# Local attention layers: output projection of two units at once over 256 columns, the norm's squares in the tile of the scaled rows, another order of the step

## The chip, the cores and the metric

The kernel runs on one core of one Trainium2 chip. The time is device microseconds of one execution of the whole program; lower is better. The core has TensorE (PE, matmuls, with its weight loads shown as PEld), VectorE (DVE), ScalarE (ACT), GpSimd (POOL) and SyncE (SP), whose queue issues most of the DMAs.

## The reference

The program computes a chain of blocks on x of 16 samples x 128 tokens x 128 features, all in float32. The change lies in one of them, `_L0_ffn_ref`, a stack of six layers of local attention and feed-forward:

```python
for i in range(DEPTH):                                  # DEPTH = 6
    x = attn_layer(shift_tokens(x), Wqkv[i], q_scale[i], k_scale[i], Wo[i]) + x
    x = ffn_layer(shift_tokens(x), ln_g[i], ln_b[i], W1[i], b1[i], W2[i], b2[i]) + x

def attn_layer(x, Wqkv, qs, ksc, Wo):
    q, k, v = jnp.split(x @ Wqkv, 3, -1)                # 16 heads of 64
    q = l2norm(sh(q)) * qs;  k = l2norm(sh(k)) * ksc    # then rotary with a scale
    out = local_attention(q, k, v)                      # windows of 32, softmax(8 q k + mask)
    return out.transpose(0, 2, 1, 3).reshape(b, n, INNER) @ Wo

def ffn_layer(x, g, bln, W1, b1, W2, b2):
    xn = (x - mu) / jnp.sqrt(var + 1e-05) * g + bln
    a, gate = jnp.split(xn @ W1 + b1, 2, -1)            # 341 each
    return a * jax.nn.gelu(gate) @ W2 + b2
```

`shift_tokens` moves the upper half of the features down by one token. Before this stack stand a conditioned attention and a warp of the images, behind it a diffusion step, a gated linear attention and two mixtures of experts; none of them is touched.

## The kernel before

x lies transposed in SBUF as `xs`: features on the 128 partitions, the 16 samples and their tokens along the row. The shift costs nothing, since the upper 64 partitions are read one column further on (`Local.halves`). A **unit** (`Unit`) is one sample in one layer, so there are 6 x 16 = 96. A **feed-forward** (`FeedForward`) takes four samples at once, 512 columns.

What a unit does, piece by piece, with the lines of the profile:

- `project(k,c)` (L774): half of the queries (k = 0) or keys (k = 1), 512 columns, from `xs` by the layer's `wqkv`. Each is read by `square` (L779, ACT, into `sq`) and `cossin` (L787, DVE, times cosine and sine into `t`); `sum_squares` (L797, DVE), `lengths` (L803 and the power of L804, POOL), `rotate` (two adds at L811, POOL, into `rot`) and `normalize_keys` (L816, POOL) follow.
- `transpose(k,c)` (L838, PE) and `keep_transpose` (L843, ACT) bring four pairs of heads into `qkT`.
- `scores(half)` (L855, PE, eight heads, into a tile of the ring "s"), `mask` (L862, DVE, in place), `maxima` (the reduction of L869 and a small multiply at L874 of 128x8 by 128x8, both in SBUF; DVE), `exponentials` (L882, ACT, one ACTIVATE per head), `normalize` (reciprocal L889 on DVE, multiply L890 on POOL).
- `values(c)` (L823, PE) with `keep_values` (L830, ACT).
- `turn(i)` (L896, PE, transposes four heads of `pe`) with `keep_turn` (L903, into `pT`: on ACT for i = 1, else on DVE), `weigh(half)` (L910, PE), `keep_weighed(half)` (L918, ACT, into `oT`), then `out` (L926, PE, eight matmuls of 128 columns that add up) and `add` (L934, DVE, two adds of 64x128 into `xs`). Every float32 matmul is two instructions in the trace, a transpose is one.

The feed-forward: `mean` (L947, PE), `center` (L951, DVE, into `xc`), `square` (L957, ACT, into `sqc`), `variance` (L963, PE), `root` (L970 on DVE, the power of L971 on POOL), `spread` (two DMAs on SP: four roots per token go to DRAM and come back broadcast to all partitions), `scale` (L985, DVE, into `xn`), `up(c)` (L993, PE), `gelu(c)` (L1001, ACT), `gate(c)` (L1009, DVE), `down` (L1017, PE) and `add` (L1023, DVE).

Psum is handed out in two rings by `Local.ps`: "s", two tiles of 1024 columns, for the scores, and "g", four tiles of 512 columns, for everything else. The tiles of a ring are given out in the order of the calls, so a piece that takes a "g" tile waits until the tile four calls earlier has been read. SBUF tiles of one name go round in the same way, with the number of buffers that the first argument of `tile` gives (`xc`, `xn`, `sqc`: one; `oT`, `v`, `qkT`, `ge`: two; `pe`, `pT`: four).

The order is written out by hand: with `manual_schedule` for PE, DVE, ACT and POOL, every engine gets its instructions in the order in which the pieces are called. `STEP` (L1031) lists the pieces of one step and `run_layers` (L1117) calls it once per four units. In a step that starts at unit n, p0 to p3 are units n to n+3, t0 to t3 are units n-2 to n+1, o0 to o3 are units n-3 to n; f is the feed-forward of the four samples before (`mean`, `center`, `square`), and e, g and h are the one of eight units before (`variance` to `scale`; `up`, `gelu`, `gate`; `down`, `add`). So a unit passes through two steps and a feed-forward through two. `FIRST` (L1075) is the list for n = 0. The DMAs of SP and the DMA waits lie outside of the written order.

## Time and profile before

| | us |
|---|---|
| three runs | 2558.02, 2558.49, 2556.04; median 2558.02 |
| the profiled execution, its own time | 2561.24 |
| its span in the profile | 2559.3 |
| first and last `out` matmul (L926) of the local layers | 494.0 and 2208.2 |
| one step in the middle of the layers | 71.0 |

Some groups of instructions between 650 and 2220 us (count, mean ns of one):

| line, engine, what | count | mean ns |
|---|---|---|
| L926 PE matmul, 128 columns | 1392 | 275 |
| L934 DVE add, 64x128 | 174 | 279 |
| L918 ACT copy into `oT`, 128x512 | 174 | 601 |
| L957 ACT square into `sqc`, 128x512 | 22 | 679 |
| L874 DVE multiply, 128x8 | 172 | 786 |
| table load ahead of L1001 and of L882, ACT | 22 and 22 | 1283 |
| L804 POOL power, 128x32 | 85 | 5676 |
| L890 POOL multiply, 128x1024 | 172 | 1897 |

How to read it: the mean ns of one matmul is its whole passage, and matmuls overlap, so the pace of PE is read from the distance between starts or from the chain of waits. A line of the profile's windows or groups counts an engine as busy while an instruction is in it, also when that instruction only waits inside. The profiled execution is 3 us above the median of the runs.

### The profile page before, as it was taken

To read this page: it belongs to the slowest core of one execution; us is meant where nothing else is said; L and a number is where in the kernel's file an instruction comes from. 1 tells how busy PE (TensorE), PEld (TensorE's weight loads), DVE (VectorE), ACT (ScalarE), POOL (GpSimd) and SP (SyncE) were. 2 spreads that over 40 slices of the span, in tenths; PEclk is the share of its full clock that TensorE was granted. 3 is DMA by queue.
4 is the path that set the end of the run, shared out by engine and by line. 5 is a ranking of instruction groups with operands and counts; after the bars stand their busy time and mean duration, and the time that the engine had idled before them with its cause. 6 is when DMAs were issued, how large, how long until landed. Compare 5 with 4: busy or idle time off the path is not lost.

```text
span 2559.3 us, 47602 instructions
## 1 busy us (share of the span) xinstructions
PE 2427.9 (95%) x17644; PEld 1671.2 (65%) x17644; DVE 2210.8 (86%) x2961; ACT 1925.6 (75%) x5717; POOL 1999.7 (78%) x1242
## 2 busy tenths in 40 slices
PE   7999998899999999999999999999999999789998
PEld 5676765566666666666666666666666766456766
DVE  5899998899999989999999989999899998455544
ACT  4788887688888878888888888888888888344422
POOL 3777777899999989999999999999999999243210
PEclk9999999999999999999999999999999999899999
DMA  3111113000000000100001000100000000022220
GB/s 107 29 31 32 28 31 109 13 1 6 13 30 16 6 13 1 38 8 6 13 8 38 6 13 1 38 8 6 5 5 5 5 6 1 11 77 68 85 71 25
DMA packets 89487, 64.73 MB, mean 25 GB/s; under 512 B 56802, under 2 KB 75944, under 8 KB 88488
## 3 DMA queue, kind: packets, MB, share of 16 engines
q1 hardware_dynamic: 78280, 37.56, 5.9%
q0 software_dynamic: 9216, 22.03, 2.8%
q8 instruction: 140, 2.29, 0.4%
q10 hardware_dynamic: 1760, 2.10, 0.2%
q14 instruction: 91, 0.75, 0.1%
HBM read 55.06 MB, written 6.60 MB: 24 GB/s over the span
## 4 chain that ended last, share of the span: by engine, by line
PE 55%; DVE 11%; ACT 6%; issue 1%; POOL 1%; DMA 1%; DVEq 0%; POOLq 0%; ACTq 0%; SPq 0%
PE g L774 9%; PE s L855 6%; PE g L910 5%; PE g L838 5%; PE g L993 5%; PE g L823 4%; PE g L896 4%; PE g L926 4%; ACT pe L882 3%; DVE t L787 2%; DVE nm L869 2%; PE e L1531 2%; DVE ss L797 1%; PE o L1549 1%; DVE nm L874 1%
## 5 line engine op out<-in xcount | busy, mean ns | idle before, releaser
L882 ACT ACTIVATE pe<-s,nm,r 128x128 f32<-128x128 f32 x1536 | 683.2, 485 | 2.4 <-DVE nm L874 1.8
L804 POOL TENSOR_TENSOR r<-ss,power 128x32 f32<-128x32 f32 x96 | 543.7, 5663 | 8.0
L811 POOL TENSOR_TENSOR rot<-t 128x512 f32<-128x512 f32 x384 | 481.9, 1276 | 20.8 <-DVE t L787 20.6
L787 DVE TENSOR_TENSOR t<-g,tab 128x1024 f32<-128x1024 f32 x372 | 447.0, 1215 | 38.9 <-PE g L774 28.5
L890 POOL TENSOR_TENSOR pe<-pe,den 128x1024 f32<-128x1024 f32 x192 | 363.2, 1897 | 49.5 <-DVE den L889 46.2
L774 PE MATMUL g<-wqkv,xs 128*128 128x512 f32 x744 | 377.5, 606 | 0.6 <-DVE t L787 0.4
L882 ACT ACTIVATION_READ_ACCUMULATOR pe<-s,nm,r 128x1 f32 x1536 | 356.4, 232 | 0.0
L779 ACT ACTIVATE sq<-g 128x512 f32<-128x512 f32 x372 | 223.9, 609 | 94.1 <-PE g L774 84.0
L843 ACT COPY qkT<-g 128x512 f32<-128x512 f32 x384 | 219.9, 614 | 61.3 <-PE g L838 60.7
L862 DVE TENSOR_TENSOR s<-s,band 128x1024 f32<-128x1024 f32 x192 | 234.6, 1222 | 16.7 <-PE s L855 16.2
L838 PEld LDWEIGHTS g<-ident,rot 128*128 128x128 f32 x1536 | 175.1, 142 | 105.4 <-issue 44.7
L896 PEld LDWEIGHTS g<-ident,pe 128*128 128x128 f32 x1536 | 179.7, 141 | 98.4 <-issue 86.8
L838 PE MATMUL g<-ident,rot 128*128 128x128 f32 x1536 | 226.3, 281 | 16.1 <-ACT qkT L843 9.1
L869 DVE TENSOR_REDUCE nm<-s 128x8 f32<-128x1024 f32 x192 | 232.7, 1212 | 0.9
L797 DVE TENSOR_REDUCE ss<-sq 128x16 f32<-128x1024 f32 x192 | 231.5, 1206 | 2.4 <-ACT sq L779 0.3
L855 PE MATMUL s<-qkT,qkT 64*128 64x128 f32 x3072 | 223.1, 285 | 3.8 <-ACT qkT L843 1.9
L855 PEld LDWEIGHTS s<-qkT,qkT 64*128 64x128 f32 x3072 | 186.3, 187 | 61.8 <-issue 51.5
L896 PE MATMUL g<-ident,pe 128*128 128x128 f32 x1536 | 223.0, 276 | 0.9 <-POOL pe L890 0.9
L903 DVE COPY pT<-g 128x512 f32<-128x512 f32 x288 | 192.5, 682 | 16.8 <-PE g L896 13.0
L823 PE MATMUL g<-wqkv,xs 128*128 128x512 f32 x384 | 203.1, 611 | 0.0
L910 PE MATMUL g<-pT,v 128*64 128x128 f32 x3072 | 199.8, 277 | 0.8 <-DVE pT L903 0.8
L926 PEld LDWEIGHTS g<-oT,wo 128*128 128x128 f32 x1536 | 182.7, 192 | 23.4 <-issue 16.7
(341 smaller groups left out, 4799.9 us busy)
## 6 DMA issues: line engine op xcount, KB each, us to landing
wqkv<-in_lo_wqkv_dram SPq DMA_DIRECT2D x6, 1536.0 KB
roots<-lo_roots SPq DMA_DIRECT2D x24, 256.0 KB
fr_image<-xres SPq DMA_DIRECT2D x32, 104.0 KB
wo<-in_lo_wo_dram SPq DMA_DIRECT2D x6, 512.0 KB
box<-fr_image,idx POOLq DMA_INDIRECT x128
fr_moved<-out SPq DMA_DIRECT2D x16, 128.0 KB
w<-in_lo_w_dram SPq DMA_DIRECT2D x6, 341.0 KB
wqk<-in_a_wqk_dram ACTq DMA_DIRECT2D x4, 256.0 KB
```

The lines of the kernel that those rows point to most:

```text
L774: self.nc.tensor.matmul(pq, self.xT, self.w.qkv[:, at : at + 512], start=True, stop=True)
L787: self.nc.vector.tensor_tensor(self.t[k][:, :, 8 * c : 8 * c + 8, :], heads(self.bank["q", k, c]).unsqueeze(1).to_broadcast([P, 2, 8, 64]) ...
L804: self.nc.gpsimd.tensor_tensor(self.r, self.ss, self.lo.power, ALU.pow)
L811: self.nc.gpsimd.tensor_tensor(self.rot[k][:, :, at], t[:, 0, :, at], t[:, 1, :, other], ALU.add)
L823: self.nc.tensor.matmul(pv, self.xT, self.w.qkv[:, 2048 + c * 512 : 2560 + c * 512], start=True, stop=True)
L838: self.nc.tensor.transpose(pt[:, j * P : j * P + P], flat[:, at : at + P], self.s.ident)
L855: self.nc.tensor.matmul(sc[:, k * 512 + j * P : k * 512 + j * P + P], self.T[0][rows, pr, :], self.T[1][rows, pr, :], start=True, stop=True,)
L882: self.nc.scalar.activation(self.pe[half][:, h, :], sc3[:, h, :], AF.Exp, bias=self.nm[half][:, h : h + 1], scale=self.r[:, hd : hd + 1], ...
L890: self.nc.gpsimd.tensor_tensor(pe, pe, den.unsqueeze(2).to_broadcast([P, 8, P]), ALU.mult)
L896: self.nc.tensor.transpose(pt[:, j * P : j * P + P], self.pe[i // 2][:, 4 * (i % 2) + j, :], self.s.ident)
L910: self.nc.tensor.matmul(po[rows, j * P : (j + 1) * P], self.v[:, hd * 64 : hd * 64 + 64], self.pT[2 * half + k][:, j, :], start=True, stop ...
L926: self.nc.tensor.matmul(self.pout[:, 0:P], self.w.o[:, c, :], self.oT[:, c, :], start=(c == 0), stop=(c == 7),)
```

## The change

`out` and `add` move from the unit to a new class `Pair` of two units: `oT` gets a place for both units (8 x 2 x 128 columns instead of 8 x 128), `out` runs eight matmuls of 256 columns, and `add` writes 64x256. `FeedForward.square` puts its squares into the tile `xn`, which `scale` writes later; `sqc` is gone. `STEP` is replaced as a whole; x0 is the pair of units n-4 and n-3, x1 that of n-2 and n-1. 

```diff
@@ -913,25 +913,35 @@
                 )
 
     def keep_weighed(self, half):
-        if half == 0:
-            self.oT = self.lo.tile(2, "oT", [P, 8, P])
+
+        pair = self.pair
+        if pair.oT is None:
+            pair.oT = self.lo.tile(2, "oT", [P, 8, 2, P])
         self.nc.scalar.copy(
-            self.oT[:, 4 * half : 4 * half + 4, :].rearrange("p c t -> p (c t)"),
-            self.bank["o", half],
-        )
+            pair.oT[:, 4 * half : 4 * half + 4, self.b % 2, :],
+            self.bank["o", half].rearrange("p (c t) -> p c t", c=4),
+        )
+
+
+class Pair:
+
+
+    def __init__(self, lo, w, b):
+        self.lo, self.nc, self.w, self.b, self.oT = lo, lo.nc, w, b, None
 
     def out(self):
         self.pout = self.lo.ps("g")
         for c in range(8):
             self.nc.tensor.matmul(
-                self.pout[:, 0:P], self.w.o[:, c, :], self.oT[:, c, :],
-                start=(c == 0), stop=(c == 7),
+                self.pout[:, 0:256], self.w.o[:, c, :],
+                self.oT[:, c].rearrange("p i t -> p (i t)"), start=(c == 0), stop=(c == 7),
             )
 
     def add(self):
-        for rows, x in self.lo.halves(self.b, 1):
-            x = x.rearrange("p i t -> p (i t)")
-            self.nc.vector.tensor_tensor(x, self.pout[rows, 0:P], x, ALU.add)
+        for rows, x in self.lo.halves(self.b, 2):
+            self.nc.vector.tensor_tensor(
+                x, self.pout[rows, 0:256].rearrange("p (i t) -> p i t", i=2), x, ALU.add
+            )
 
 
 class FeedForward:
@@ -953,7 +963,7 @@
         )
 
     def square(self):
-        self.sq = self.lo.tile(1, "sqc", [P, 512])
+        self.sq = self.xn = self.lo.tile(1, "xn", [P, 512])
         self.nc.scalar.activation(self.sq, self.xc, AF.Square)
 
     def variance(self):
@@ -981,7 +991,6 @@
         )
 
     def scale(self):
-        self.xn = self.lo.tile(1, "xn", [P, 512])
         self.nc.vector.tensor_tensor(
             four(self.xn), self.roots.rearrange("p t i -> p i t"), four(self.xc), ALU.mult
         )
...
 STEP = """
-t0.transpose(1,0) p0.project(0,0) t0.keep_transpose(1,0) p0.cossin(0,0) t0.transpose(0,0)
-p0.project(0,1) p0.project(1,0) t0.keep_transpose(0,0) p0.square(0,0) p0.square(1,0)
-p0.cossin(0,1) p0.square(0,1) t0.scores(0) t1.transpose(0,0) t1.keep_transpose(0,0)
-t1.transpose(0,1) t1.keep_transpose(0,1) o0.turn(1) p0.cossin(1,0) t0.mask(0) o0.turn(3)
-t0.transpose(1,1) o0.keep_turn(1) o0.keep_turn(3) t0.transpose(0,1) t0.values(0)
-t0.keep_transpose(1,1) t0.maxima(0) o0.turn(0) o0.keep_turn(0) o0.turn(2) t0.keep_transpose(0,1)
-p0.project(1,1) o0.keep_turn(2) p0.cossin(1,1) p0.sum_squares(0) t0.keep_values(0) t0.values(1)
-e.variance() t0.scores(1) e.root() t0.exponentials(0) t0.mask(1) p0.square(1,1) p0.rotate(0)
-o0.weigh(0) t0.normalize(0) o0.weigh(1) t0.keep_values(1) t1.transpose(1,0) o0.keep_weighed(0)
-o0.keep_weighed(1) p1.project(0,0) t1.keep_transpose(1,0) p1.square(0,0) t0.maxima(1)
-p0.rotate(1) o0.out() p0.sum_squares(1) p1.project(0,1) p1.cossin(0,0) o0.add() t1.values(0)
-p1.cossin(0,1) e.spread() t0.exponentials(1) o1.turn(0) o1.keep_turn(0) p1.square(0,1)
-t1.scores(0) t1.keep_values(0) e.scale() t1.transpose(1,1) t1.keep_transpose(1,1) t1.mask(0)
-o1.turn(1) p1.sum_squares(0) o1.keep_turn(1) g.up(2) t1.maxima(0) g.gelu(2) g.up(1) g.gelu(1)
-t1.scores(1) g.gate(2) o1.weigh(0) p0.lengths() g.gate(1) t0.normalize(1) t1.mask(1) g.up(0)
-p1.project(1,0) t1.maxima(1) o1.keep_weighed(0) g.gelu(0) p1.project(1,1) p1.square(1,0)
-p0.normalize_keys() g.gate(0) p1.square(1,1) o1.turn(3) p1.cossin(1,0) p1.rotate(0)
-p1.cossin(1,1) h.down() o1.keep_turn(3) t2.transpose(0,0) t2.transpose(1,0) h.add()
-t1.exponentials(0) p1.sum_squares(1) p2.project(1,0) p2.square(1,0) p2.project(1,1) p1.rotate(1)
-p1.lengths() t2.keep_transpose(0,0) t1.normalize(0) t2.transpose(0,1) p2.cossin(1,0)
-t2.keep_transpose(1,0) p2.square(1,1) t2.keep_transpose(0,1) p2.cossin(1,1) t2.transpose(1,1)
-o1.turn(2) t2.keep_transpose(1,1) o1.keep_turn(2) t2.scores(0) t2.values(0) t1.exponentials(1)
-p2.project(0,0) t2.mask(0) o1.weigh(1) t2.keep_values(0) p2.cossin(0,0) t1.normalize(1)
-t1.values(1) p2.project(0,1) p2.square(0,0) o1.keep_weighed(1) t1.keep_values(1)
-p1.normalize_keys() t2.maxima(0) t3.transpose(0,0) p2.sum_squares(1) t2.scores(1) p2.square(0,1)
-o2.turn(0) p2.cossin(0,1) p2.rotate(0) t2.values(1) t2.mask(1) t3.keep_transpose(0,0)
-t2.exponentials(0) o2.keep_turn(0) t2.keep_values(1) o2.turn(1) t2.maxima(1) o2.keep_turn(1)
-o1.out() t2.normalize(0) o1.add() t3.transpose(1,0) o2.turn(3) t3.keep_transpose(1,0) o2.turn(2)
-t3.transpose(0,1) t3.scores(0) t2.exponentials(1) p2.sum_squares(0) o2.keep_turn(3) p2.rotate(1)
-t3.keep_transpose(0,1) o2.keep_turn(2) o2.weigh(0) t3.mask(0) t2.normalize(1) o2.weigh(1)
-o2.keep_weighed(0) t3.transpose(1,1) p3.project(1,0) o2.keep_weighed(1) p3.project(0,0)
-o3.turn(1) t3.keep_transpose(1,1) t3.maxima(0) p3.square(0,0) t3.scores(1) o3.turn(2)
-p2.lengths() o3.keep_turn(1) p3.cossin(1,0) p3.cossin(0,0) t3.mask(1) o3.keep_turn(2)
-p3.square(1,0) p3.project(1,1) o3.turn(0) p3.square(1,1) p3.cossin(1,1) o2.out() t3.values(0)
-o3.keep_turn(0) o3.turn(3) o2.add() p3.rotate(1) o3.weigh(0) t3.exponentials(0) o3.keep_turn(3)
-t3.keep_values(0) p3.project(0,1) o3.weigh(1) o3.keep_weighed(0) p3.square(0,1) t3.maxima(1)
-f.mean() p2.normalize_keys() t3.normalize(0) p3.sum_squares(0) p3.cossin(0,1) o3.keep_weighed(1)
-o3.out() f.center() t3.values(1) o3.add() p3.rotate(0) t3.exponentials(1) t3.keep_values(1)
-p3.sum_squares(1) t3.normalize(1) p3.lengths() f.square() p3.normalize_keys()
+p0.project(1,0) p0.project(1,1) p0.cossin(1,0) t0.transpose(0,0) p0.square(1,0) p0.project(0,0)
+p0.cossin(1,1) p0.project(0,1) p0.square(1,1) t0.transpose(1,0) t0.keep_transpose(0,0)
+p0.cossin(0,0) p0.square(0,0) t1.transpose(0,0) t0.transpose(1,1) p0.rotate(1)
+t0.keep_transpose(1,0) p0.cossin(0,1) t0.scores(0) t1.keep_transpose(0,0) p0.square(0,1)
+p0.sum_squares(1) t1.transpose(0,1) t0.keep_transpose(1,1) t1.keep_transpose(0,1) t0.values(0)
+t0.keep_values(0) t0.transpose(0,1) t0.mask(0) t0.maxima(0) p0.sum_squares(0)
+t0.keep_transpose(0,1) t1.transpose(1,0) t1.transpose(1,1) t1.keep_transpose(1,0) o0.turn(0)
+t1.keep_transpose(1,1) o0.turn(2) e.variance() o0.keep_turn(2) p0.rotate(0) t0.scores(1)
+t0.exponentials(0) o0.keep_turn(0) o0.turn(1) e.root() p1.project(0,0) t0.mask(1) p1.cossin(0,0)
+o0.keep_turn(1) t0.values(1) t0.keep_values(1) p1.square(0,0) p1.project(1,0) t2.transpose(0,0)
+p0.lengths() t0.maxima(1) p1.square(1,0) o0.turn(3) t0.normalize(0) t1.scores(1) o0.weigh(0)
+p1.cossin(1,0) e.spread() p1.project(1,1) t2.keep_transpose(0,0) t0.exponentials(1) t1.mask(1)
+o0.keep_weighed(0) o0.keep_turn(3) t1.values(0) p1.cossin(1,1) t1.maxima(1) o0.weigh(1)
+p1.project(0,1) p0.normalize_keys() p1.square(1,1) t1.values(1) t1.keep_values(0) p1.square(0,1)
+t1.scores(0) o0.keep_weighed(1) t0.normalize(1) o1.turn(1) e.scale() o1.turn(0)
+t1.keep_values(1) p1.cossin(0,1) t1.mask(0) t2.transpose(0,1) o1.keep_turn(0) o1.keep_turn(1)
+p1.sum_squares(1) t2.transpose(1,0) o1.turn(3) p1.rotate(1) t2.keep_transpose(0,1) o1.turn(2)
+t2.keep_transpose(1,0) o1.weigh(0) o1.keep_turn(3) p1.sum_squares(0) p1.rotate(0)
+p2.project(1,0) t1.maxima(0) o1.keep_turn(2) t1.exponentials(1) p1.lengths() p2.square(1,0)
+o1.keep_weighed(0) x0.out() t3.transpose(0,0) p2.project(0,0) t1.exponentials(0) p2.cossin(1,0)
+t2.transpose(1,1) x0.add() t1.normalize(1) p2.project(1,1) t3.keep_transpose(0,0) t2.scores(0)
+p2.cossin(0,0) p2.square(0,0) p2.project(0,1) p2.cossin(1,1) t3.transpose(0,1) t1.normalize(0)
+t2.keep_transpose(1,1) t2.mask(0) p2.square(1,1) p2.square(0,1) p2.cossin(0,1) g.up(1)
+t3.keep_transpose(0,1) g.gelu(1) o1.weigh(1) p2.rotate(1) t2.maxima(0) p1.normalize_keys()
+t2.scores(1) o1.keep_weighed(1) o2.turn(3) p2.sum_squares(0) g.gate(1) t2.exponentials(0)
+o2.turn(2) p2.rotate(0) o2.keep_turn(3) o2.turn(0) o2.turn(1) p2.sum_squares(1) o2.keep_turn(1)
+o2.keep_turn(2) p3.project(1,0) o2.keep_turn(0) t3.transpose(1,0) p3.cossin(1,0) p3.project(0,0)
+p3.square(1,0) o2.weigh(0) p3.square(0,0) o2.weigh(1) t2.mask(1) t3.keep_transpose(1,0)
+p3.project(1,1) p3.cossin(0,0) p2.lengths() t2.normalize(0) o2.keep_weighed(0) t3.transpose(1,1)
+o2.keep_weighed(1) p3.square(1,1) t2.maxima(1) p3.project(0,1) t3.keep_transpose(1,1)
+p3.cossin(1,1) t2.values(0) p3.square(0,1) t2.exponentials(1) p3.cossin(0,1) t3.scores(0)
+g.up(0) g.gelu(0) t3.mask(0) p3.sum_squares(1) g.gate(0) x1.out() t2.keep_values(0)
+p2.normalize_keys() t2.normalize(1) t3.values(0) x1.add() p3.sum_squares(0) t3.maxima(0) g.up(2)
+t2.values(1) t3.keep_values(0) g.gelu(2) g.gate(2) o3.turn(1) t2.keep_values(1) t3.scores(1)
+o3.turn(2) t3.mask(1) o3.keep_turn(2) o3.turn(3) t3.maxima(1) o3.keep_turn(1) f.mean()
+t3.exponentials(0) o3.turn(0) o3.keep_turn(3) f.center() o3.keep_turn(0) h.down() t3.values(1)
+o3.weigh(0) o3.weigh(1) h.add() p3.rotate(1) p3.rotate(0) t3.exponentials(1) t3.keep_values(1)
+o3.keep_weighed(0) p3.lengths() t3.normalize(0) o3.keep_weighed(1) f.square()
+p3.normalize_keys() t3.normalize(1)
 """.split()
...
@@ -1085,8 +1094,8 @@
 t3.keep_values(0) t3.maxima(0) o3.turn(3) o3.keep_turn(1) p3.rotate(1) t3.exponentials(0)
 p3.rotate(0) o3.keep_turn(0) t3.mask(1) o3.turn(2) o3.weigh(0) o3.keep_weighed(0) t3.values(1)
 o3.keep_turn(3) t3.keep_values(1) o3.keep_turn(2) o3.weigh(1) t3.maxima(1) o3.keep_weighed(1)
-p3.sum_squares(0) p3.sum_squares(1) t3.exponentials(1) t3.normalize(0) o3.out() o3.add()
-t3.normalize(1) p3.lengths() p3.normalize_keys()
+p3.sum_squares(0) p3.sum_squares(1) t3.exponentials(1) t3.normalize(0) t3.normalize(1)
+p3.lengths() p3.normalize_keys()
 """.split()
...
@@ -1116,7 +1125,7 @@
 
 def run_layers(lo, early):
     total = DEPTH * B
-    layers, units, ffs = lo.layers, lo.units, {}
+    layers, units, pairs, ffs = lo.layers, lo.units, {}, {}
     for n in range(0, total + 12, 4):
         L, b = divmod(n, B)
         if n < total:
@@ -1127,9 +1136,14 @@
                 layers[L + 1].gains()
             for i in range(4):
                 units.setdefault(n + i, Unit(lo, layers[L], b + i))
+            for i in (0, 2):
+                pairs[n + i] = units[n + i].pair = units[n + i + 1].pair = Pair(
+                    lo, layers[L], b + i
+                )
             ffs[n] = FeedForward(lo, layers[L], b)
         at = {"f": ffs.get(n - 4)}
         at["e"] = at["g"] = at["h"] = ffs.get(n - 8)
+        at["x0"], at["x1"] = pairs.get(n - 4), pairs.get(n - 2)
         for i in range(4):
             for who, behind in (("p", 0), ("t", 2), ("o", 3)):
                 at[f"{who}{i}"] = units.get(n + i - behind)

```

## The prediction

> **What bounds the kernel now.** First the page's totals and the whole span in slices, then busy time per engine in stretches of one step, then the chain of waits inside one step, then two short stretches of the timeline. The local layers run from about 490 to 2236 us of 2559.3, and TensorE (PE) is the busiest engine.
>
> ```profile
> span 2559.3 us, 47602 instructions
> PE 2427.9 (95%) x17644; PEld 1671.2 (65%) x17644; DVE 2210.8 (86%) x2961; ACT 1925.6 (75%) x5717; POOL 1999.7 (78%) x1242
> ...
> PEclk9999999999999999999999999999999999899999
> ```
>
> The granted clock is full, so a clock change is not what this edit can win. The stretches of 71 us each hold one call of STEP; the columns are busy us of PE, PE's weight loads, DVE, ACT and POOL, each with its count, then clock, DMA share and GB/s.
>
> ```profile
> 1361.00:1432.00 71.00, 70.31 (x524) 48.20 (x523) 67.94 (x84) 60.51 (x187) 66.76 (x37) 1.00 0.06 15
> 1432.00:1503.00 71.00, 70.31 (x524) 48.09 (x523) 67.91 (x85) 60.50 (x186) 66.75 (x38) 1.00 0.03 5
> ...
> 1929.00:2000.00 71.00, 70.31 (x523) 48.00 (x522) 67.94 (x83) 60.50 (x187) 66.97 (x37) 1.00 0.02 5
> ```
>
> The same numbers each time: the step is periodic at 71.0 us, and PE, DVE and POOL are all within 5 us of it. Any order is therefore bounded by how the three interlock, not by one of them. The chain of waits shows where (start, duration, what ran):
>
> ```profile
> 1398.12 1.73 PE g L774 x4
> ...
> 1400.49 1.28 ACT L882
> ...
> 1401.79 3.63 ACT pe L882 x16
> 1405.42 0.49 ACT sq L779
> 1405.90 0.48 ACT qkT L843
> ...
> 1406.43 1.15 PE g L838 x8
> ...
> 1411.20 1.22 DVE t L787
> ...
> 1418.98 1.03 DVE nm L874
> ```
>
> For some 50 us of a step the chain is PE alone; then it goes through ACT (the 1.28 us table load for exp after the three gelus, then exponentials) and some 9.5 us of DVE. The last line is odd: an 8-column multiply that takes 1.03 us. The timeline of DVE and POOL explains it (start, duration, engine):
>
> ```profile
> 1372.46 5.45 POOL L804 TENSOR_TENSOR r<-ss,power 128x32 f32<-128x32 f32 x1
> 1376.95 0.17 DVE L874 TENSOR_TENSOR nm<-nm,r 128x8 f32<-128x8 f32 x1
> ...
> 1397.74 1.90 POOL L816 TENSOR_TENSOR rot<-rot,r 128x1024 f32<-128x1024 f32 x1
> 1398.13 1.53 DVE L874 TENSOR_TENSOR nm<-nm,r 128x8 f32<-128x8 f32 x1
> ```
>
> L874 reads two tiles of SBUF. Begun inside POOL's L816 it ends with it (1399.66 against 1399.64); begun inside the power of L804 it takes 0.17. The step's eight L874 hold 6.2 us, so about 4.9 us (6.2 - 8 x 0.17) is this wait.
>
> **The change, part by part.** *Output projection.* Per unit, 16 matmuls of 128 columns take 1.78 us in the chain. Two instructions of 512 columns take 0.86 us (a project), 0.84 ns a column and instruction, so 16 of 256 columns take at least 3.44; at most 2 x 1.78 = 3.56 if nothing is gained. I take 3.48, nearer the per-column row, as the weight load (192 ns) still fits under a 215 ns matmul. Gain 0.08 a pair, 0.16 us of PE a step. The eight adds of 64x128 go in pairs at 0.58 us; a 64x256 add lies between one of those (0.29) and the 64x512 form of L1023 (0.75): I take 0.42 (0.29 + 128 x 1.04 ns, the slope from 64x128 to L862's 1222 ns for 1024 columns), 0.80 a pair against 1.16: 0.7 us of DVE a step (0 to 1.2). keep_weighed writes the same 512 columns with a stride: 0.60, taken as unchanged (0 to +0.1, ACT, 10 us idle a step). *Squares in xn's place.* f.square must now wait for the last g.up of its step to have read xn. In the new order that is g.up(2), 10 us of PE before f.square: nothing; without that cover ACT would wait up to 10 us with the next step's squares behind it. *Ring.* Two fewer tiles of the four-deep "g" ring a step. *SP.* e.spread's two DMAs go with e.root; they get about 10 us before e.scale where they had 7.1 (1382.07 to 1389.19): nothing.
>
> *The order.* This is the large part. t0, t1, o1 and so on are the units of one step. I lay the new list end to end with the durations of the rows (pitch: project and values 0.86, transposes 0.45, scores 1.09, weigh 0.98, up 1.75, down 2.6; DVE: L787, L797, L862 1.13, L869+L874 1.41, pT copy 0.60, scale 1.0, gate 0.67, reciprocal 0.13; ACT: 512-column ops 0.49, eight exponentials 3.49, load 1.28; POOL: 1.27, 1.90, 5.46). Pure PE work is 68.4 us before and 68.3 after; changes of matmul shape make the old step some 0.9 longer (69.3), so it holds 1.7 us of stalls. That is the most that a perfect order could gain: 1.7 + 0.2.
>
> The new list has three stretches:
> 1. From the step's first PE work to o1.turn(2). It begins with four projections, and before o1.turn(2) the ring needs o1.keep_turn(0). DVE waits 0.95 us for the first project and then has 23.9 us of work up to the end of that copy: 8 L787, 4 L862 and 2 L797 (14 x 1.13), 3 maxima (4.2), 4 pT copies (2.4), the scale, 2 reciprocals and the root (1.4). Against PE's 25.6 that fits only if L874 never waits. But t1.maxima(1)'s multiply comes about 9 us after e.root, and POOL, which starts its root at the same moment, is then past the power (1.0+0.3+5.5) and inside the L890 and L816 that follow: it waits to the end of L816, about 1.4; t0.maxima(0) meets p0.rotate: about 0.6. So 26.9 us (25.3 to 28), PE late by 1.3.
> 2. To o2.turn(2), whose bank needs g.gate(1): 14.8 us of DVE (4 L787, 3 L797, 1 L862, 2 maxima, 2 copies, x0.add, 2 reciprocals, the gate), plus 1.0 of waits of two more L874 (0 to 2) and 0.3 of waiting for the projects that are now late: 16.1, against PE's 15.0.
> 3. To the end PE leads: 27.7 pure, 0.4 for shape changes, 0.2 at p3.project(0,0).
>
> Sum 26.9 + 16.1 + 28.3 = 71.3. Laid along its own chain with these pitches (49.4 us of PE, 6.2 of ACT, 4.2 of PE, 9.6 of DVE) the old step gives 69.4; 1.0 of the missing 1.6 are shape changes, which the third stretch already has, and 0.6 are small gaps, of which I add some 0.2, since two of the new stretches are DVE's, where the pitches were exact: 71.5 against 71.0. The bounds of the waits make it 69.9 to 73.6.
>
> *Table loads.* In the new list gelu(1) stands between t1's and t2's exponentials and gelu(0), gelu(2) between t2's and t3's. The instruction order of the built kernels has 89 loads on L1010/L882 where it had 47: 42 more x 1.28 = 53.9 us of ACT. Per step ACT goes from 60.5 to 63.1 of 71. The first extra load sits between o1.weigh(1) and t2.exponentials(0), on whose heels o2.keep_turn(1) and o2.weigh(0) wait: from the end of g.up(1) ACT needs 0.6+0.5+1.28+3.49+0.49 = 6.4, PE has 6.0 of work and stretch 2's lateness, which covers the rest. The second sits ahead of g.gate(0), which stalls DVE about 1.7 us where PE has x1.out (3.48) to do. I price them 0, with cover; 2 x 1.28 x 21 = 54 without.
>
> The Trainium skill, page "ScalarE: Activation LUTs", sections "Rules for kernel authors" and "What ACT_TABLE_LOAD costs", advises to do all work of one table set before switching to another, and gives 1283 ns plus a drain of about 1380 ns for each switch. That speaks against this order. The trace has the 1283 but no drain of that size (the exponential starts 0.01 us after the load); by the page's 2.66 us the 42 loads would be an estimated 112 us of ACT. The page "SBUF — State Buffer", section "Who interferes with whom", says that a DVE instruction with two SBUF inputs is blocked for the whole of a GpSimd instruction that reads SBUF; the L816 row agrees, the L804 row does not; by the rule t0.maxima(1), inside the power, would wait an estimated 3 us more a step.
>
> *Sum.* 22 full steps x 0.5 = 11; in the draining steps x1.out holds the path for 3.48 where o2.out held it for 1.78, plus the larger add: 2. Profiled 2559.3 + 13 = 2572 in span; the profiled run was 2561.24 and the median 2558.02, 3 us less, so 2571.
>
> **The rivals.** *A, the forecast:* DVE leads in the first 43 us of the step; step 71.2 to 72.0, 2562 to 2582. For it: L874's anchoring to e.root; against: 1 us of DVE waits decides it. *B, faster:* POOL runs a little earlier or later and L874 meets powers or gaps; then PE leads throughout, and the step is 69.2 to 70.7. From 0.8 us less wait in stretches 1 and 2 than I count, it is faster. Middle 70.2: -0.8 x 22 + 2 = -16, 2542. For it: 0.7 us less DVE and 0.2 less PE; against: nothing in the trace lets DVE start its step before the first project. *C, the loads show:* both extra loads land on the chain, as the one at 1400.49 does: 71.0 + 2.4, +53 + 2, about 2612. For it: that line; against: the ten idle us of ACT. *D, no change* (within 0.2%, 5 us, about what a measurement can tell here): step 70.7 to 71.1.
>
> **How the numbers follow.** A 0.42, B 0.32, C 0.13, D 0.13. A and C are slower: 0.55; B faster: 0.32; D same: 0.13. A's own range is 2562 to 2582; ten times in ten would need 2520 to 2615. For eight in ten I leave out the lower third of B (0.10) and the upper half of C (0.07): 2540 to 2604.
>
> **What would show it.** Right: steps of 71.2 to 72.0, L874 still near 0.75 us in the mean, DVE in the chain for the first 43 us of the step, PE idle before o1.turn(2) and o2.turn(2) for DVE L903 and L1009; 16 out matmuls in about 3.48 us, DVE busy about 67; 89 loads off the chain. Wrong: a step under 70.7 with a PE chain (B), table loads in the chain with PE waiting for ACT at o2.weigh(0) (C), or an out pair over 3.6.

## The result and the profile after

| | before | after |
|---|---|---|
| median (range), us | 2558.26 (2556.04 to 2558.49) | 2624.22 (2620.56 to 2628.49), four runs |
| ratio, 95% interval | | 1.0262 [1.025, 1.0275] |
| span of the profiled execution | 2559.3 | 2622.7 |
| first to last f.square (L957, L967), 23 steps | 1645.3 | 1707.4 |
| a step inside a layer (median of the 23) | 71.35 | 75.05 |
| the last of the 23, which drains the layers | 47.5 | 43.0 |

The change is slower by 2.6%, and 62.1 of the 63.4 us between the two spans lie in these 23 steps (66.6 more in the first 22, 4.5 less in the last). What the prediction called "periodic at 71.0" is 71.35, from one f.square to the next. The step that ends a layer also prepares the weights of the next one; it takes 74.4 to 84.0 us in the kernel before and 74.9 to 87.9 in the changed one.

The page of the changed kernel: totals, the granted clock in slices, shares of the chain of waits.

```profile
span 2622.7 us, 46186 instructions
...
PE 2454.2 (94%) x16876; PEld 1655.9 (63%) x16876; DVE 2153.2 (82%) x2865; ACT 1984.5 (76%) x5759; POOL 1985.5 (76%) x1242
...
PEclk9999999999999989999999999999999999989999
...
PE 60%; DVE 11%; POOL 8%; issue 2%; ACT 1%; DMA 1%; DVEq 0%; POOLq 0%; ACTq 0%; SPq 0%
```

PE has 768 instructions fewer and is busy 26 us longer, DVE 58 us shorter. Two steps in stretches of 75.05 us (busy us and count of PE, weight loads, DVE, ACT, POOL; then clock, DMA share, GB/s):

```profile
1349.00:1424.05 75.05, 72.40 (x493) 47.73 (x492) 66.57 (x82) 63.85 (x190) 66.54 (x38) 0.98 0.10 32
1424.05:1499.10 75.05, 72.39 (x493) 47.75 (x492) 66.60 (x81) 63.76 (x190) 66.55 (x38) 0.98 0.04 7
```

The clock was 1.00 in the steps of before and is 0.98 here. No engine carries 3.7 us more work (ACT has 3.3 more, mostly the two loads, and idles 11 us a step), so PE waits, and for a while it runs slowly. The chain of waits in the second of these steps (start, duration, what ran):

```profile
1423.98 1.22 DVE t L787
...
1426.37 1.21 DVE nm L874
...
1430.92 0.60 DVE pT L903
...
1431.57 0.66 PE g L896 x4
...
1434.30 3.45 PE g L935 x16
...
1451.54 0.27 POOL ss L803
...
1451.87 1.05 PE g L838 x4
1452.92 1.71 PE g L774 x2
1454.63 2.26 PE g L910 x32
```

The first lines are the stretch led by DVE that was forecast. The last three are new: 4 transposes take 1.05 us (0.63 elsewhere behind a gap), two matmuls of a project 1.71 (0.86), 32 of weigh 2.26 (1.90), in sum 1.63 us more. PE's timeline at that place (start, duration, what, idle time ahead of it and its releaser by the profile) and the stretches around it show why:

```profile
1448.50 1.11 PE L774 MATMUL g<-wqkv,xs 128*128 128x512 f32 x2
1451.87 1.05 PE L838 MATMUL g<-ident,rot 128*128 128x128 f32 x4 [2.26 <-POOL ss L803]
```

```profile
1449.00:1452.00 3.00, 0.74 (x3) 0.16 (x2) 3.00 (x5) 2.75 (x13) 2.92 (x5) 0.99 0.01 3
1452.00:1455.00 3.00, 3.00 (x10) 1.50 (x11) 1.02 (x1) 0.91 (x2) 3.00 (x1) 0.50 0.02 5
1455.00:1458.00 3.00, 3.00 (x37) 2.30 (x33) 2.60 (x4) 1.93 (x5) 3.00 (x2) 0.94 0.00 0
```

PE stands still for 2.26 us ahead of t3.transpose(1,0), and then the granted clock is halved. The gap is there in 22 steps, 2.25 to 2.28 us each; behind 17 of them come 3.41 us at half clock.

### The profile page after: what moved, and what is told of

Same layout as the page of the kernel before. It is cut to its first block, busy times and chain, and to the rows that moved or that the text cites. A ratio compares the mean times of both kernels' runs of the same rounds, so it can differ in the third digit from the quotient of the medians.

```text
span 2622.7 us, 46186 instructions
## 1 busy us (share of the span) xinstructions
PE 2454.2 (94%) x16876; PEld 1655.9 (63%) x16876; DVE 2153.2 (82%) x2865; ACT 1984.5 (76%) x5759; POOL 1985.5 (76%) x1242
## 4 chain that ended last, share of the span: by engine, by line
PE 60%; DVE 11%; POOL 8%; issue 2%; ACT 1%; DMA 1%; DVEq 0%; POOLq 0%; ACTq 0%; SPq 0%
PE g L774 11%; PE g L935 6%; PE g L910 6%; PE g L838 6%; PE s L855 5%; PE g L823 5%; POOL rot L811 4%; PE g L896 4%; DVE t L787 4%; PE g L1002 3%; PE g L1026 2%; DVE s L862 2%; POOL pe L890 2%; POOL rot L816 2%; PE e L1545 2%
## 5 line engine op out<-in xcount | busy, mean ns | idle before, releaser
L804 POOL TENSOR_TENSOR r<-ss,power 128x32 f32<-128x32 f32 x96 | 525.0, 5469 | 8.0
L811 POOL TENSOR_TENSOR rot<-t 128x512 f32<-128x512 f32 x384 | 478.4, 1275 | 10.2 <-DVE t L787 10.0
L890 POOL TENSOR_TENSOR pe<-pe,den 128x1024 f32<-128x1024 f32 x192 | 377.2, 1970 | 137.2 <-DVE den L889 130.3
L774 PE MATMUL g<-wqkv,xs 128*128 128x512 f32 x744 | 409.3, 643 | 4.6 <-ACT sq L779 3.3
L838 PEld LDWEIGHTS g<-ident,rot 128*128 128x128 f32 x1536 | 180.7, 143 | 179.1 <-issue 74.8
L910 PEld LDWEIGHTS g<-pT,v 128*64 128x64 f32 x3072 | 178.7, 145 | 93.4 <-issue 38.1
L855 PEld LDWEIGHTS s<-qkT,qkT 64*128 64x128 f32 x3072 | 186.3, 187 | 74.4 <-issue 64.5
L896 PE MATMUL g<-ident,pe 128*128 128x128 f32 x1536 | 213.0, 277 | 7.5 <-DVE pT L903 6.4
L910 PE MATMUL g<-pT,v 128*64 128x128 f32 x3072 | 214.0, 290 | 3.5 <-DVE pT L903 3.5
L896 PEld LDWEIGHTS g<-ident,pe 128*128 128x128 f32 x1536 | 170.5, 140 | 49.6 <-issue 24.6
L823 PE MATMUL g<-wqkv,xs 128*128 128x512 f32 x384 | 197.2, 595 | 0.8 <-DVE pT L903 0.8
```

Of the source, the lines that this page charges most:

```text
L774: self.nc.tensor.matmul(pq, self.xT, self.w.qkv[:, at : at + 512], start=True, stop=True)
L804: self.nc.gpsimd.tensor_tensor(self.r, self.ss, self.lo.power, ALU.pow)
L811: self.nc.gpsimd.tensor_tensor(self.rot[k][:, :, at], t[:, 0, :, at], t[:, 1, :, other], ALU.add)
L823: self.nc.tensor.matmul(pv, self.xT, self.w.qkv[:, 2048 + c * 512 : 2560 + c * 512], start=True, stop=True)
L838: self.nc.tensor.transpose(pt[:, j * P : j * P + P], flat[:, at : at + P], self.s.ident)
L855: self.nc.tensor.matmul(sc[:, k * 512 + j * P : k * 512 + j * P + P], self.T[0][rows, pr, :], self.T[1][rows, pr, :], start=True, stop=True,)
```

## What ends the gap

Two things end just before PE goes on at 1451.87. POOL's L803 ends 0.06 us earlier, and the profile names it. ACT's o2.keep_turn(1) ends 0.14 us earlier, at 1451.73; ACT's queue there is (start, duration, what):

```profile
1443.63 1.28 ACT L1010 ACT_TABLE_LOAD   x1
1444.92 0.69 ACT L1010 ACTIVATE ge<-g,b1n 128x512 f32<-128x512 f32 x1
1445.72 0.58 ACT L920 COPY oT<-g 128x512 f32<-128x512 f32 x1
1446.33 1.28 ACT L882 ACT_TABLE_LOAD   x1
...
1451.12 0.61 ACT L903 COPY pT<-g 128x512 f32<-128x512 f32 x1
```

The theory: t3.transpose(1,0) gets the psum tile of o2.turn(1), which o2.keep_turn(1) reads; tiles of a ring are given out in the order in which the list frees them. In the changed list o2.keep_turn(1) stands ahead of o2.keep_turn(2) and o2.keep_turn(0); in time it ends last, since those two run on DVE and end by 1450.8. The rival is POOL, which holds rotated keys back.

**e1_no_first_switch**: the changed kernel with an exponential in the place of gelu(1), which leaves out this gelu and the table loads around it, 47 loads in all.

```diff
-             self.ge[c][0:n], self.pg[c, 1][0:n], AF.Gelu,
+             self.ge[c][0:n], self.pg[c, 1][0:n], AF.Exp if c == 1 else AF.Gelu,
```

> The changed kernel with gelu(1) computed as an exponential instead of a Gelu (part of the feed-forward is computed wrongly): the order of every engine is the same, only two of the four table loads of a step are gone. Theory A (PE's gap of 2.3 us ahead of t3.transpose(1,0) waits for ACT's o2.keep_turn(1), which stands behind the load and t2.exponentials(0), and the gap then halves PE's clock for about 3.4 us): ACT reaches keep_turn(1) some 1.5 us earlier, the gap shrinks to under 1 us, the clock stays at 1.00, the step falls from 75.05 to 71 to 72 us, the time to about 2545 to 2560. Theory B (the gap waits for POOL, as the profile's releaser L803 says): the gap stays over 2 us and the time within 10 us of 2624. Theory C (the forecast's DVE stretches are what costs): no change beyond 10 us.

Measured: 2570.07 us, ratio 1.0056 [1.0039, 1.0072], step 72.03; the step is at the upper end of theory A's, the time 10 us above its range. The gap is 0.84 to 0.87, and it still ends with ACT's copy (PE's timeline of e1_no_first_switch):

```profile
1348.55 0.63 PE L838 MATMUL g<-ident,rot 128*128 128x128 f32 x4 [0.86 <-ACT pT L903]
```

**e2_bank_order**: the changed kernel with its 89 loads; one copy moved in the list, so that another psum tile is free first. No engine's own order changes in the steps.

```diff
-o2.turn(2) p2.rotate(0) o2.keep_turn(3) o2.turn(0) o2.turn(1) p2.sum_squares(1) o2.keep_turn(1)
-o2.keep_turn(2) p3.project(1,0) o2.keep_turn(0) t3.transpose(1,0) p3.cossin(1,0) p3.project(0,0)
+o2.turn(2) p2.rotate(0) o2.keep_turn(3) o2.turn(0) o2.turn(1) p2.sum_squares(1) o2.keep_turn(2)
+p3.project(1,0) o2.keep_turn(0) o2.keep_turn(1) t3.transpose(1,0) p3.cossin(1,0) p3.project(0,0)
```

> The changed kernel with o2.keep_turn(1) called after o2.keep_turn(2), p3.project(1,0) and o2.keep_turn(0): no engine's own order changes, but t3.transpose(1,0) gets the psum tile that DVE frees with keep_turn(2) instead of the one that ACT frees with keep_turn(1), and o2.weigh(0) gets ACT's. Theory A: t3.transpose(1,0) and p3.project(0,0) (1.3 us) run before ACT is done, the gap splits into pieces under 1.2 us, no half clock; the step is 71.5 to 72.5, the time 2555 to 2580. Theory B: unchanged, 2615 to 2630, since nothing on POOL moves. Theory C: unchanged.

Measured: 2566.0 us, ratio 1.0042 [1.0029, 1.0055], step 71.99; 58 of the 66 us are back. ACT's queue has hardly moved, PE's has (ACT, then PE, in the timeline of e2_bank_order):

```profile
1340.41 1.28 ACT L882 ACT_TABLE_LOAD   x1
...
1345.20 0.61 ACT L903 COPY pT<-g 128x512 f32<-128x512 f32 x1
```

```profile
1342.58 1.09 PE L774 MATMUL g<-wqkv,xs 128*128 128x512 f32 x2
1344.37 0.63 PE L838 MATMUL g<-ident,rot 128*128 128x128 f32 x4 [0.69 <-DVE pT L903]
1344.87 1.13 PE L774 MATMUL g<-wqkv,xs 128*128 128x512 f32 x2
```

From the load for exp to the copy behind the exponentials ACT takes 4.79 us here and took 4.79 in the changed kernel (1446.33 to 1451.12). But the transposes now start 0.8 us before that copy, and in the changed kernel they started behind it. In the built program the matmuls of t3.transpose(1,0) wait on ACT and POOL in the changed kernel, on DVE and POOL in this one. So the wait is for the psum tile, shown by moving nothing else.

**e3_keys_first**: the changed kernel with POOL's keys earlier.

```diff
-t3.keep_transpose(0,1) g.gelu(1) o1.weigh(1) p2.rotate(1) t2.maxima(0) p1.normalize_keys()
+t3.keep_transpose(0,1) g.gelu(1) o1.weigh(1) p1.normalize_keys() p2.rotate(1) t2.maxima(0)
```

> The changed kernel with p1.normalize_keys ahead of p2.rotate(1) on POOL, so that the keys which t3.transpose(1,0) reads are ready some 2.5 us earlier. Theory A: the gap still ends with ACT's keep_turn(1); time 2615 to 2635. Theory B: the gap shrinks to under 1 us and the time falls by 50 us or more, to below 2575. Theory C: within 10 us of 2624.

Measured: 2631.92 us, ratio 1.0288 [1.0271, 1.0305], step 75.46. POOL's order moved, the gap stayed, and the profile names another releaser (PE's timeline of e3_keys_first):

```profile
1381.20 0.63 PE L838 MATMUL g<-ident,rot 128*128 128x128 f32 x4 [2.06 <-ACT pT L903]
```

POOL as the cause falls. The run also gives the price of the half clock by itself: three steps inside a layer, in which the clock didn't fall, take 73.83 to 73.84 us, the others 75.35 to 75.50, so a fall costs 1.6 us.

**e4_old_order**: the paired projection and the shared tile in the order of before; x0 stands in o0's place, x1 in o2's, the pieces of o1 and o3 go.

```diff
-p0.rotate(1) o0.out() p0.sum_squares(1) p1.project(0,1) p1.cossin(0,0) o0.add() t1.values(0)
+p0.rotate(1) x0.out() p0.sum_squares(1) p1.project(0,1) p1.cossin(0,0) x0.add() t1.values(0)
...
-o1.out() t2.normalize(0) o1.add() t3.transpose(1,0) o2.turn(3) t3.keep_transpose(1,0) o2.turn(2)
+t2.normalize(0) t3.transpose(1,0) o2.turn(3) t3.keep_transpose(1,0) o2.turn(2)
...
-p3.square(1,0) p3.project(1,1) o3.turn(0) p3.square(1,1) p3.cossin(1,1) o2.out() t3.values(0)
-o3.keep_turn(0) o3.turn(3) o2.add() p3.rotate(1) o3.weigh(0) t3.exponentials(0) o3.keep_turn(3)
+p3.square(1,0) p3.project(1,1) o3.turn(0) p3.square(1,1) p3.cossin(1,1) x1.out() t3.values(0)
+o3.keep_turn(0) o3.turn(3) x1.add() p3.rotate(1) o3.weigh(0) t3.exponentials(0) o3.keep_turn(3)
...
-o3.out() f.center() t3.values(1) o3.add() p3.rotate(0) t3.exponentials(1) t3.keep_values(1)
+f.center() t3.values(1) p3.rotate(0) t3.exponentials(1) t3.keep_values(1)
```

> The old order of the step with the two other parts of the change: pairs of units for out and add (x0 in the place of o0.out, x1 in that of o2.out), squares in xn. Theories A, B and C alike: the loss lies in the order, so this is not slower than before; 0.2 us of PE and 0.7 us of DVE less a step, of which up to 0.7 shows on the chain: 2540 to 2560, table loads 47. If the paired projection itself costs: over 2570.

Measured: 2619.73 us, ratio 1.0242 [1.0225, 1.0259], step 73.93. That is 60 us above what was expected: with 47 loads and the old order the pair costs almost as much as the whole change. The reason is looked for below.

## What is left, and whether the causes add up

**e5_squares_only**: the kernel before, with its own output projection and list, and only the squares in the tile `xn` (the two lines of `FeedForward` from the change).

> The kernel before with the squares of the norm put into xn, and nothing else. e4 (pairs and squares in the old order) took 73.93 us a step where before took 71.35. If the pairs cost that (3.46 us of PE in one piece where ACT and DVE had 1.78), this is within 6 us of before, 2551 to 2563, the step 71.35. If the shared tile costs it (f.square waiting for the last g.up, or g.up for variance), this takes 2600 or more.

Measured: 2556.54 us, ratio 0.9996 [0.9984, 1.0007], step 71.34. The shared tile costs nothing.

**f2_bank_and_switch**: e1's and e2's edits together.

> e2 with gelu(1) computed as an exponential, as in e1 (part of the feed-forward is computed wrongly). Each alone took the step from 75.05 to 72.0. If both removed the same thing (PE's long wait ahead of t3.transpose(1,0) and the half clock behind it), the two together give little more: step 71.6 to 72.0, 2555 to 2568. If they were separate losses, the step falls by another 2 us or more, to below 2530.

Measured: 2565.27 us, ratio 1.0029 [1.0016, 1.0042], step 71.89. The two don't add: each alone takes away the same gap and the half clock behind it. The extra load matters only because the copy that frees the tile stands behind it.

**f1_bank_scale**: e2, and e.scale behind the two copies that free tiles for o1, because a gap of 0.40 us ahead of o1.turn(2) is left in the stretch led by DVE.

```diff
-t1.scores(0) o0.keep_weighed(1) t0.normalize(1) o1.turn(1) e.scale() o1.turn(0)
-t1.keep_values(1) p1.cossin(0,1) t1.mask(0) t2.transpose(0,1) o1.keep_turn(0) o1.keep_turn(1)
+t1.scores(0) o0.keep_weighed(1) t0.normalize(1) o1.turn(1) o1.turn(0)
+t1.keep_values(1) p1.cossin(0,1) t1.mask(0) t2.transpose(0,1) o1.keep_turn(0) o1.keep_turn(1) e.scale()
```

> e2 with e.scale moved on DVE from ahead of p1.cossin(0,1) to behind o1.keep_turn(0). In e2 PE stands 0.40 us ahead of o1.turn(2), which waits for o1.keep_turn(0) at the end of a DVE stretch that holds the 0.96 us of e.scale; the later stretch has 0.65 us of DVE idle. Forecast's stretch 1: the 0.40 goes, the step is 71.5 to 71.7, the time 2553 to 2561. If DVE's sum over both stretches is what binds: no change, 2563 to 2569.

Measured: 2572.69 us, ratio 1.0051 [1.0034, 1.0068], step 72.1, neither of the two that were expected. The gap of 0.40 is gone, and a load with the exponentials of two halves behind it (7.15 us) leads the chain at another place of the step.

**g1_no_switch_at_all**: f1 with exponentials in the place of all three gelus, so that no gelu and no load is left in the steps.

> f1 with all three gelus computed as exponentials (the feed-forward's gate is computed wrongly): no table load in the local layers. In f1 the gap ahead of o1.turn(2) was gone, but the load ahead of t3's exponentials (1.28 us) and the exponentials led the chain into the next step, at 72.1 us. If the second switch is what binds there, the step falls by 0.6 to 1.3 us, to 70.8 to 71.5: 2540 to 2558. If DVE's or PE's sum binds, it stays at 71.9 to 72.1: 2562 to 2575.

Measured: 2564.02 us, ratio 1.0021 [1.0011, 1.003], step 72.09. Without any load the new order is still not faster than before. In its chain DVE leads for a part, and e.scale (L994), put at this place, takes 1.91 us in the median where it takes 1.04 in the changed kernel. The traces show what it meets there (timeline of POOL and DVE in g1_no_switch_at_all, then in the changed kernel):

```profile
1400.20 5.71 POOL L811 TENSOR_TENSOR rot<-t 128x512 f32<-128x512 f32 x4
1401.69 1.91 DVE L994 TENSOR_TENSOR xn<-roots,xc 128x512 f32<-128x512 f32 x1
```

```profile
1427.61 1.04 DVE L994 TENSOR_TENSOR xn<-roots,xc 128x512 f32<-128x512 f32 x1
1427.84 2.52 POOL L890 TENSOR_TENSOR pe<-pe,den 128x1024 f32<-128x1024 f32 x1 [0.28 <-PE g L823]
```

In g1 it begins inside one of POOL's adds of `rotate` (L811) in 22 of 24 cases and ends 0.88 to 0.90 us behind the end of that add; the add after it takes 2.0 us instead of 1.27. In the changed kernel nothing runs on POOL when it begins. So moving e.scale won PE's 0.40 us at the price of a longer e.scale.

## Why the pair costs in the old order

In e4_old_order PE stands still for 1.04 us each step ahead of the next step's p0.project(0,1) and for 0.59 ahead of o2.turn(2) (PE's timeline of e4_old_order):

```profile
1300.26 0.66 PE L896 MATMUL g<-ident,pe 128*128 128x128 f32 x4 [0.59 <-ACT v L830]
...
1323.21 2.13 PE L774 MATMUL g<-wqkv,xs 128*128 128x512 f32 x4 [1.04 <-ACT v L830]
```

Four more kernels moved the pair and its add.

**f4_pair_late**: e4 with x0 in the place of o1.

```diff
-p0.rotate(1) x0.out() p0.sum_squares(1) p1.project(0,1) p1.cossin(0,0) x0.add() t1.values(0)
+p0.rotate(1) p0.sum_squares(1) p1.project(0,1) p1.cossin(0,0) t1.values(0)
...
-t2.normalize(0) t3.transpose(1,0) o2.turn(3) t3.keep_transpose(1,0) o2.turn(2)
+x0.out() t2.normalize(0) x0.add() t3.transpose(1,0) o2.turn(3) t3.keep_transpose(1,0) o2.turn(2)
```

> As e4 (pairs and squares in the old order), but x0.out and x0.add stand in the places of o1.out and o1.add, half a step later. In the kernel before the chain is PE alone from t3.transpose(0,1) over the end of the step to p1.project(1,1); three of the four outs lie in it (3 x 1.78 us), in e4 both pairs (2 x 3.46), here only x1.out. If the place of the 3.46 us decides what a pair costs, PE's stretch is 1.9 us shorter than before, the other stretch takes x0.out in PE's idle time, and the step is 69.6 to 71.2 against 71.35: 2518 to 2554, faster than before. If the pair costs wherever it stands (its psum tile and its adds held twice as long), the step stays at 73 to 74: over 2590.

Measured: 2616.24 us, ratio 1.0223 [1.0208, 1.0239], step 73.51: the second of the two holds. PE's gaps in one step (timeline; of f4_pair_late, then of the kernel before):

```profile
1321.32 2.13 PE L774 MATMUL g<-wqkv,xs 128*128 128x512 f32 x4 [1.05 <-ACT v L830]
...
1341.26 3.64 PE L1002 MATMUL g<-xn,w1n 128*85 128x512 f32 x8 [0.61 <-DVE xn L994]
...
1357.23 1.14 PE L838 MATMUL g<-ident,rot 128*128 128x128 f32 x8 [0.37 <-ACT qkT L843]
```

```profile
1406.43 1.15 PE L838 MATMUL g<-ident,rot 128*128 128x128 f32 x8 [0.42 <-ACT qkT L843]
...
1420.73 0.63 PE L838 MATMUL g<-ident,rot 128*128 128x128 f32 x4 [0.18 <-DVE xs L934]
```

These gaps are 2.03 us a step against 0.60. Each of the two new ones stands a few pieces behind a place where the list of before had an output projection: o3.out, then p0.project(0,1); o0.out, then g.up. Counted from start to start of PE's instructions over one step, idle time has grown by 1.62 us (0.69 to 2.31), projects and values by 0.47, transposes by 0.27, and the output projection has shrunk by 0.23. That is 2.13 of the 2.16 us by which the step grew.

**f5_pair_behind_weigh** and **f6_pair_early_behind_weigh** put x1 into o3's place, so that the gap of 1.05 should close, with x0 in o1's place and in o0's; f.mean and f.center follow it.

```diff
-o3.out() f.center() t3.values(1) o3.add() p3.rotate(0) t3.exponentials(1) t3.keep_values(1)
+x1.out() t3.values(1) x1.add() f.mean() f.center() p3.rotate(0) t3.exponentials(1) t3.keep_values(1)
```

> The step list of before with the paired projection and the shared tile; x0.out()/x0.add() stand where o1.out()/o1.add() stood, x1.out()/x1.add() where o3.out()/o3.add() stood (behind o3.weigh(1)), and f.mean() f.center() follow x1.add(). 47 table loads. Theory (in f4_pair_late it is the place of x1 that costs: with nothing between o3.weigh(1) and t3.values(1), PE waits about 1 us a step for keep_values(1), which stands behind the sixteen exponentials on ACT): now the pair covers that time, the wait of PE ahead of the next step's first project is gone, step 70.8 to 71.6 us, 2535 to 2570 us. Rival (an out of 3.46 us in one piece costs wherever it stands in the old order, because the copies and exponentials that PE's next pieces need are late by as much): step 72.5 to 74, 2590 to 2625.

> As f5_pair_behind_weigh, but x0.out()/x0.add() where o0.out()/o0.add() stood. Theory: what costs is x1's place; the place of x0 matters by less than 0.4 us a step (e4_old_order against f4_pair_late: 73.93 against 73.51), so within 10 us of f5_pair_behind_weigh, 2540 to 2580. Rival (any place costs): 2595 to 2630.

Measured: 2624.85 us, 1.0251 [1.0232, 1.027], step 73.50, and 2638.62 us, 1.0299 [1.0281, 1.0318], step 74.39. The theory falls in both; f5 lies in the rival's range, f6 9 us above it. The gap of 1.05 is gone in both, and others stand behind the places that are empty now (PE's timeline of f5_pair_behind_weigh, then of f6_pair_early_behind_weigh):

```profile
1312.54 1.09 PE L910 MATMUL g<-pT,v 128*64 128x128 f32 x16 [0.95 <-DVE pT L903]
...
1342.76 3.64 PE L1002 MATMUL g<-xn,w1n 128*85 128x512 f32 x8 [0.61 <-DVE xn L994]
```

```profile
1315.00 0.66 PE L896 MATMUL g<-ident,pe 128*128 128x128 f32 x4 [0.59 <-ACT v L830]
...
1328.11 1.09 PE L910 MATMUL g<-pT,v 128*64 128x128 f32 x16 [1.17 <-DVE pT L903]
```

In these orders DVE also stood idle ahead of the pair's add, for 44 to 59 us in 40 cases (0.9 us before). Is that the cost? **f7_add_behind_work** is f4 with work put ahead of both adds.

```diff
-x0.out() t2.normalize(0) x0.add() t3.transpose(1,0) o2.turn(3) t3.keep_transpose(1,0) o2.turn(2)
+x0.out() t2.normalize(0) t3.transpose(1,0) o2.turn(3) t3.keep_transpose(1,0) o2.turn(2)
...
-t3.keep_transpose(0,1) o2.keep_turn(2) o2.weigh(0) t3.mask(0) t2.normalize(1) o2.weigh(1)
+t3.keep_transpose(0,1) o2.keep_turn(2) x0.add() o2.weigh(0) t3.mask(0) t2.normalize(1) o2.weigh(1)
...
-o3.keep_turn(0) o3.turn(3) x1.add() p3.rotate(1) o3.weigh(0) t3.exponentials(0) o3.keep_turn(3)
-t3.keep_values(0) p3.project(0,1) o3.weigh(1) o3.keep_weighed(0) p3.square(0,1) t3.maxima(1)
+o3.keep_turn(0) o3.turn(3) t3.maxima(1) x1.add() p3.rotate(1) o3.weigh(0) t3.exponentials(0) o3.keep_turn(3)
+t3.keep_values(0) p3.project(0,1) o3.weigh(1) o3.keep_weighed(0) p3.square(0,1)
```

> f4_pair_late (step 73.51 us, 2616.24 us) with DVE's queue alone rearranged around the two pairs: x0.add() behind o2.keep_turn(3) and o2.keep_turn(2) instead of right behind t2.normalize(0), and t3.maxima(1) ahead of x1.add(). The same instructions, PE's order the same, 47 table loads. In f4_pair_late DVE stands idle for 0.84 us ahead of x0.add() and for 1.40 us ahead of x1.add(), until the last matmul of the pair (44.5 us in 40 cases between 700 and 2200 us; before: 0.9 us). Theory (what an output projection of 3.46 us in one piece costs in the old order is this idle time of DVE, whose queue stands still behind an add that follows its matmuls directly): idle time ahead of L942 under 10 us, step 71.3 to 72.4 us, 2562 to 2592 us. Rival (the length of the pair delays o3.weigh and the exponentials by itself, and DVE's idle time is only its shadow): the idle time moves to other lines, step 73.0 to 73.8, 2603 to 2622.

Measured: 2615.74 us, 1.0212 [1.0194, 1.023]. The idle time ahead of L942 is gone altogether, and nothing is won: PE's gaps are those of f4 (f7_add_behind_work, PE's timeline).

```profile
1320.77 2.13 PE L774 MATMUL g<-wqkv,xs 128*128 128x512 f32 x4 [1.04 <-ACT v L830]
...
1340.71 3.64 PE L1002 MATMUL g<-xn,w1n 128*85 128x512 f32 x8 [0.61 <-DVE xn L994]
...
1356.68 1.14 PE L838 MATMUL g<-ident,rot 128*128 128x128 f32 x8 [0.38 <-ACT qkT L843]
```

DVE's idle time was only the shadow. The four placements (e4, f4, f5, f6) are the four ways to keep one of the places of o0.out and o1.out and one of those of o2.out and o3.out, and in each a gap opens behind both empty places: 0.61 ahead of g.up without o0.out (f4, f5), 0.59 ahead of o2.turn(2) without o1.out (e4, f6), 0.95 and 1.17 ahead of o3.weigh(0) without o2.out (f5, f6), 1.04 and 1.05 ahead of p0.project(0,1) without o3.out (e4, f4). This fits the reading that four projections of 1.78 us gave PE work at four places while ACT or DVE caught up, and that two of 3.46 leave two of these places bare. It isn't shown that the moving alone does it: no kernel moved single projections to the places of the pairs, and none had the new order with single projections. In the four placements the cost was 2.1 to 3.0% (with f7); that no placement in the old order is free wasn't shown either. The new order avoids most of this (e2: 0.4%), but no version with the pair beats the kernel before.

## Why the prediction was wrong

The sign was right; 2571 was 53 us too low, and the range ended 20 us below the result.

The loss has another cause than the one forecast; that the time grows at all holds without it too (e2: 0.4%).

*The projection.* Right: 3.45 us for the 16 matmuls (3.48 said), 0.86 for the two adds (0.80). *Squares.* Right by e5.

*Stretches one and two.* Right in length: from the step's first PE work (1404.1, one step before 1479.18) to o1.turn(2) at 1431.57 are 27.4 us, 26.9 said, and from there to o2.turn(2) 15.6, 16.1 said. In the first one PE does wait at its end for o1.keep_turn(0), the last piece of DVE's chain. But "DVE in the chain for the first 43 us" didn't come: PE leads for 20 us, then DVE for 7.5, and in stretch two PE is busy throughout and doesn't wait ahead of o2.turn(2), so that its length came out near the forecast partly by luck. t1.maxima(1)'s L874 took 1.21, of which 1.04 is the wait (1.4 said): in it POOL runs L816, 1425.65 to 1427.55, and L874 ends at 1427.58. Over the step L874 fell further than said, to 0.53 us in the mean (0.75 said); the 2 us of DVE so won changed nothing that shows, as DVE leads only at places.

*The step of 71.5.* Nearly right once the failed step is out of it: e2 has the same orders on every engine and all 89 loads, at 71.99 us (71.2 to 72.0 said), 0.64 above the 71.35 of before where 0.5 was said. Stretch three, with PE in the lead, was to take 28.3 us; it takes 28.9 in e2 and 31.9 in the changed kernel, so the whole loss lies in it. The "1.7 us of stalls" of the old step were too many: from start to start of its instructions PE is idle for 0.69 us of the 71.35, so a better order had less to win. The lower bound of 69.9 leaves out the 1.0 by which the waits in stretch two could have been less. The draining steps were off: +2 said, but the last of the 23 steps is 4.5 us shorter than before (43.0 against 47.5), and behind it the spans differ by 0.5.

*Table loads, second.* Right. DVE waits 1.68 us ahead of the gate (DVE's timeline, changed kernel), and PE has no gap there:

```profile
1465.42 0.75 DVE L1018 SCALAR_TENSOR_TENSOR hT<-g,b1n,ge 128x512 f32<-128x512 f32 x1 [1.68 <-ACT ge L1010]
```

*Table loads, first: this is the step that failed.* "On whose heels o2.keep_turn(1) and o2.weigh(0) wait ... ACT needs 6.4, PE has 6.0 of work and stretch 2's lateness, which covers the rest." ACT takes 7.1 us (from the end of g.up(1) at 1444.65 to 1451.73), 0.7 more than said. What failed is PE's deadline: the first that waits for o2.keep_turn(1) is not o2.weigh(0) but t3.transpose(1,0), two PE pieces earlier, for its psum tile, and up to there PE has 5.0 us (1444.65 to 1449.61). The rule behind it was wrong as well: the section on the kernel before says that a piece waits for the tile four calls earlier, and the prediction built on it. By that rule t3.transpose(1,0) gets the tile of o2.turn(2), which DVE frees in time. The waits in the built program and e2 show that here tiles are reused in the order in which the list frees them, so that where a copy stands in the list decides who waits for it, even if no engine's order changes.

*The clock.* "A clock change is not what this edit can win" overlooked that it can be lost. Between 600 and 2190 us the clock is at half for 68 us, against 17 in the kernel before and 17 in e2. Step by step against e2: the 17 of 22 steps with a fall behind the gap are 3.0 to 3.1 us longer, together 52; of the five without, four are 1.1 to 1.4 longer and one, in which e2's own clock falls, 0.2 shorter. With 0.3 in the draining step that makes the whole 57.3 us between the two kernels in the repeated steps. In a step with a fall the gap is 1.57 us longer and the slow pieces 1.63, in sum 3.2 for the 3.06 measured. The prediction had both at nothing.

*Rivals.* C came nearest (loads on the chain, 2612), but through a psum tile, not at o2.weigh(0), with one load of the two, and with a price that is half clock. "54 without cover" was close to the loss by luck: f2 shows that with the tile freed in time the first load costs 0.1 us a step.

The Trainium skill, page "TensorE: Matmul & The Clock Gate", Part 1, has a free-running window of 3413 ns by which the clock is halved and restored; the 3.41 us here agree. It also gives the practical rule that PE shouldn't be idle for more than about 3.4 us. Here 2.05 to 2.28 us were enough in 33 of 44 cases, so the measurement decides for a tighter rule.

The page "ScalarE: Activation LUTs", section "What ACT_TABLE_LOAD costs", would add a drain of about 1380 ns to each switch. No run here shows it: from the load to the exponential are 0.01 us, and f2 against e2 prices the two loads at 0.1 us a step.

## What to carry to other kernels

Where buffers are handed out in program order, ask for each piece not only whose data it reads but whose buffer it gets and which queue the reader that frees it stands in; list the frees in the order in which they will really happen. A large piece split over several places may be the filler of those places, and joining two halves is worth only what the joined piece saves, less the gaps that open. Here a wait of PE of 2 us could cost 1.6 us more in clock.
